# Two-layer relational graph convolution on one core: layer 2's root product made in layer 1, and 21 edge tiles of layer 2 brought by SyncE

## The chip, the cores and the metric

The kernel runs on one core of one Trainium2 chip. The metric is the device time of one execution in microseconds (us). The span of a profile is the time from the first to the last instruction of the profiled execution.

## The reference

The graph has 12,500 nodes with 128 features each and 200,000 edges, sorted by destination; each edge has one of 8 relations. Two layers are computed, and a residual with a layer norm at the end:

```python
def _rgcn_conv(x, src, dst, et, basis, comp, root, bias):
    W = jnp.einsum('rb,bio->rio', comp, basis)
    xw = jnp.einsum('ni,rio->nro', x, W)
    msgs = xw[src, et]
    seg = dst * N_REL + et
    summed = jax.ops.segment_sum(msgs, seg, num_segments=N_NODES * N_REL)
    cnt = jax.ops.segment_sum(jnp.ones((msgs.shape[0],), x.dtype), seg, num_segments=N_NODES * N_REL)
    mean = summed / jnp.maximum(cnt, 1.0)[:, None]
    agg = mean.reshape(N_NODES, N_REL, HIDDEN).sum(axis=1)
    return agg + x @ root + bias
h = x
for l in range(2):
    h_new = jax.nn.relu(_rgcn_conv(h, src, dst, edge_type, basis[l], comp[l], root[l], bias[l]))
    h = h_new + h
out = _layernorm(x + h)
```

The term that the change moves is `x @ root + bias` of the second layer.

## The kernel before

**Tiles, quads and blocks.** The edges are cut into 1,563 tiles of 128. Eight tiles make a quad (`Q = 8`), 196 quads in all (`NQ`). The nodes are cut into 98 blocks of 128 (`NT`). Two quads feed one block.

**Layer 1** runs over the quads `o`. GpSimd (POOL) gathers the source rows of each tile from `x` with one indirect DMA of 128 rows (`gather`, recorded at L806). TensorE multiplies the gathered rows by one-hot matrices that VectorE makes (`means`, L1364), then by the relation weights (`product`, L1396), and puts the result at its place in the block (`place`, L1427 and L1429). `finish` (L1435) adds what was carried over from the block before, makes the next carry with the bias added (L1452), and makes the new block of h with relu and residual (L1472). Each block of h is kept in `hT`, stored to `h_d` by ScalarE's DMA queue, and multiplied by the eight relation weights of layer 2 into rows of `y_d` (`table`, L1495), 51 MB in all.

**Layer 2** runs over the same quads `q`, and reads rows of `y_d`, one per edge. For 130 of the first 192 quads POOL gathers the eight tiles from `y_d`, and TensorE adds them into slots (`slot_sums`, L2026) and puts them in place one quad later (`place_sums`, L2059). The other 62 quads (`ROUTED`: 7, 10, ... 190) are done without a gather of all rows: VectorE compares lists that SyncE loads (`lo_d`, `sc_d`, L1868), TensorE picks rows out of `hT` and sums them (`pick_rows` L1918, `add_up` L1938, `relate` L1958), and POOL brings only one tile of leftovers (`gather_left`, L830). The last four quads go through `add_rows` (L2083). In `place_sums` and `add_rows` the first quad of a block also multiplies the block of h, loaded by SyncE from `h_d` two quads ahead (`open_block`, L1833), by the root weights `w_sb[:, 1, R, :]` (L2063, L2086); this is called `root_in`. The loaded block of h is also the residual in `finish`.

**What sets the order.** `Plan` writes out every engine's instructions by hand, in program order, and adds the semaphore waits that the data needs. Each engine runs its list in order. POOL's gathers are issued `AHEAD = 5` quads before they are used; the rows lie in a ring of 7 quad buffers (`rows_r`). For the last six quads (`LATE = 6`) a gather also waits for the latest sums that TensorE has done (`after`).

**Single rows.** 24 tiles of layer 1 (tile 191 and every 56th after it) aren't gathered by POOL. SyncE (SP) brings their 128 rows with one DMA of 512 bytes each (`single_rows`, L741). The row addresses come from a list in DRAM (`off_d`, made by `single_lists` at two quads, `LISTED = (14, 172)`), 32 of them by one load into SP's registers (L755), each followed by 32 row transfers (L759). A tile is split into eight chunks of 16 rows, put into SP's program at quad `(t - step - 16 + c * step / 8) // 8` for chunk `c` of tile `t`. Its two buffers (`hw_b`) alternate. SP's program also has the loads of layer 2: `fetch` and `fetch_rows` (the lists of the routed quads), `open_block`, the blocks of x, and the stores of the output.

Of the kernel before, what the change touches and what calls it, by code (L numbers as in the profile page):

```python
# [8 lines left out]
F32 = mybir.dt.float32  # L9
# [421 lines left out]
def ordered_path(  # L431
# [78 lines left out]
    NR = len(ROUTED)  # L510
    SORT = 96
    RC, RL = 16, 32
    SINGLES = [("SP", 0, range(191, NQ * Q - 80, 56))]
    SINGLE = {(l, t): (i, k) for i, (_, l, ts) in enumerate(SINGLES) for k, t in enumerate(ts)}
    LISTED = (14, NQ - 24)
    assert all(l == 0 or all(t // Q not in ROUTED and t // Q < NQ - 4 for t in ts) for _, l, ts in SINGLES)
# [13 lines left out]
    y_d = dram.tile([N * R, D], F32, name="y_d")  # L530
    w_d = dram.tile([L, R * D, D], F32, name="w_d")
    h_d = dram.tile([NT, D, P], F32, name="h_d")

    idx = keep([P, B * P], I32, "idx")
    idy = keep([P, B * P], I32, "idy")
# [137 lines left out]
    off = keep([P, B], F32, "off")  # L673
    o2 = keep([P, B], F32, "o2")
    nb_f = keep([1, 1], F32, "nb_f")

    hw_b = {e: [keep([P, D], F32, f"hw_{e}{i}") for i in range(2)] for e in {e: 0 for e, _, _ in SINGLES}}
    offs = [keep([P, len(ts)], I32, f"off{i}") for i, (_, _, ts) in enumerate(SINGLES)]
# [756 lines left out]
    def finish(l, k, apart=False):  # L1435

        n = rows_of(k)

        def first_step():
            a, ac = acc[k] if apart and k + 1 < NT else acc.pop(k)  # L1440
            emits, reads, cells = [], [ac, ("bias_t", l)], []
            if k >= 0:
                vs[k] = a, ac
            if (l, k) == (1, NT - 1):
                return
            if k >= 0:
                t, c = carry.pop(k)
                emits.append(lambda: nc.vector.tensor_add(a[:, :n], a[:, :n], t[:, :n]))  # L1448
                reads.append(c)
            if k + 1 < NT and not apart:  # L1450
                nt, ncell = carry[k + 1] = carry_r.take()
                emits.append(lambda: nc.vector.tensor_scalar(nt, a[:, P:], bias_t[:, l:l + 1], None, op0=ALU.add))  # L1452
                cells.append(ncell)

            vec(in_turn(emits), reads, cells)

        def second_step():
            if k < 0:
                return
            v, vc = vs.pop(k)  # L1460
            h = hT[:, k * P:k * P + n]
            if l == 0:
                res, rc = x_cols(k)
                o, oc = h, h_cells(k)
            else:
                ht, hc = hb.pop(k)
                res, rc = ht[:, :n], [hc]
                g = k * P // GN
                if g not in wide:
                    wide[g] = wide_r.take()  # L1470
                o, oc = wide[g][0][:, k * P % GN:k * P % GN + n], [wide[g][1] + (k,)]
            vec(lambda: nc.vector.scalar_tensor_tensor(o, v[:, :n], 0.0, res, op0=ALU.max, op1=ALU.add),  # L1472
                [vc] + rc, oc)

        def carry_step():
            if k + 1 < NT:
                a, ac = acc[k]
                nt, ncell = carry[k + 1] = carry_r.take()
                vec(lambda: nc.vector.tensor_scalar(nt, a[:, P:], bias_t[:, l:l + 1], None, op0=ALU.add),
                    [ac, ("bias_t", l)], [ncell])  # L1480

        return (first_step, second_step, carry_step)[:3 if apart else 2]


    def table(j):

        n = rows_of(j)
        yr, yrc = yr_r.take()
        split = j >= NT - 2

        def half(k, at_b=None):
            hb, bc = at_b or (s_b[k] if j == NT - 2 else ct_b if split and k == 1 else pt_b)

            def first_step():
                pe(lambda: nc.tensor.matmul(hb[:n].rearrange("p r d -> p (r d)"), hT[:, j * P:j * P + n],  # L1495
                                            w_sb[:, 1, k * H:(k + 1) * H, :].rearrange("p r d -> p (r d)"),
                                            start=True, stop=True),
                   [("h", j)] + [("w", 1, r) for r in range(k * H, (k + 1) * H)], [bc])

            def second_step(copy=copy):  # L1500
                if split and k == 1:
                    vec(lambda: nc.vector.tensor_copy(yr[:n, H:, :], hb[:n]), [bc], [yrc + (k,)])
                else:
                    copy(yr[:n, k * H:(k + 1) * H, :], hb[:n], [bc], [yrc + (k,)])
                if split:
                    load(y_d[j * P * R:(j * P + n) * R, :].rearrange("(p r) d -> p r d", r=R)[:, k * H:(k + 1) * H, :],
                         yr[:n, k * H:(k + 1) * H, :], [yrc + (k,)], [("y_d", j, k)])
                elif k == 1:
                    stores.append(lambda: load(
                        y_d[j * P * R:(j * P + n) * R, :].rearrange("(p r) d -> p (r d)", r=R),  # L1510
                        yr[:n].rearrange("p r d -> p (r d)"), [yrc + (0,), yrc + (1,)], [("y_d", j)], "ACT"))

            return first_step, second_step

        if not split:
            return [lambda at_b, k=k: half(k, at_b) for k in range(2)]
        return [half(0), half(1)]

    todo, turned_to, tables, stores, copies = [], [], [], [], []

# [312 lines left out]
    def open_block(k):  # L1833
        n = rows_of(k)
        t, c = hb_b[k % 3]
        load(t[:, :n], h_d[k][:, :n], [("h_d", k)], new(c))
        hb[k] = t, c

    def spread_of(a):
        return bass.AP(tensor=a.tensor, offset=a.offset, ap=[[0, P], *a.ap])  # L1840
# [197 lines left out]
    def place_sums(q, k, opens, last):  # L2038
        t, c = pl.pop(q)
        o, oc = ys.pop(q)  # L2040
        a, ac = acc[k]
        root_in = opens and k >= 0
        reads = [c, oc]
        m = NW if q in ROUTED else P
        if root_in:
            ht, hc = hb[k]
            reads += [hc, ("w", 1, R)]
        more = []
        if q == SOON // Q:
            reads += fix_rows_c + fix_dm_c  # L2050
            more.append((fix_rows, fix_dm))
        if q in ROUTED:
            i = ROUTED.index(q)
            (lt, lc), (ld, ldc) = left_rows_b[i % len(left_rows_b)], left_dm_b[i % 2]
            reads += [lc, ldc]
            more.append((lt, ld))

        def emit():
            ins = nc.tensor.matmul(a, o[:m], t[:m], start=opens, stop=last and not root_in and not more)  # L2059
            for rows_m, dm_m in more:  # L2060
                ins = nc.tensor.matmul(a, rows_m, dm_m, start=False, stop=last and not root_in)  # L2061
            if root_in:
                ins = nc.tensor.matmul(a[:, :rows_of(k)], w_sb[:, 1, R, :], ht[:, :rows_of(k)], start=False, stop=last)  # L2063
            return ins

        pe(emit, reads, [ac])
        plan.mark("PE")

    def add_rows(q, k, opens, last, between_last=None):
# [1 line left out]
        d, dc = dms.pop((1, q))  # L2071
        a, ac = acc[k]
        n = in_quad(q)
        root_in = opens and k >= 0
        more = []
        if root_in:
            ht, hc = hb[k][0][:, :rows_of(k)], hb[k][1]
            more += [hc, ("w", 1, R)]

        def some(i0, i1):  # L2080
            def emit():
                for i in range(i0, i1):
                    ins = nc.tensor.matmul(a, t[:, i, :], d[:, i, :],  # L2083
                                           start=(opens and i == 0), stop=(last and i == n - 1))
                    if i == 0 and root_in:
                        nc.tensor.matmul(a[:, :rows_of(k)], w_sb[:, 1, R, :], ht, start=False, stop=False)  # L2086
                return ins

            return emit

        if q == NQ - 2:
            for h in range(2):
                pe(some(4 * h, 4 * h + 4), [c + (h,)] + dc + more, [ac, ("done", 1)])
        elif q == NQ - 1:
            m = rows_of(k)
            assert opens and last and k == NT - 1
# [6 lines left out]
                pe(lambda i=i: nc.tensor.matmul(a[:, :m], t[:, i, :], d[:, i, :m], start=False, stop=i == n - 1),  # L2103
                   [c + (i,)] + dc, [ac, ("done", 1)])
        else:
            pe(some(0, n), [c + (0,), c + (1,)] + dc + more, [ac, ("done", 1)])
        plan.mark("PE")

    def first_sums():
# [187 lines left out]
    def end():  # L2297
        for k, step in ending:
            step()
            if k >= 0:  # L2300
                stores.append(lambda k=k: load(h_d[k][:, :rows_of(k)], hT[:, k * P:k * P + rows_of(k)], [("h", k)],
                                               [("h_d", k)], "ACT"))
                tables.extend(table(k))
            if k > 0 and k % TURN == TURN - 1 and k < LATER:
                tables.append(lambda at_b, k=k: turn_rows(k + 1 - TURN, *at_b))
        ending.clear()
# [8 lines left out]
    for o in range(NG - 3):  # L2315
# [37 lines left out]
        for step in behind:  # L2353
            pe(*step)
            plan.mark("PE")
        behind.clear()
        if len(tables) > 4 and (TABLE <= o < SORT - 2 or o >= SORT + NR + 4):
            a, b = tables.pop(0)(pt_b)
            a()
# [50 lines left out]
    opened.clear()  # L2410
    batch(None)
    end()
    placed(g - 4)
    product(g - 3)
    take_product(g - 3)
# [33 lines left out]
        a()  # L2449
    for _, b in halves:  # L2450
        b()

    for q in range(AHEAD):
        gather(1, q)
# [151 lines left out]
```

## Time and profile before

| what | us |
|---|---|
| median of 3 runs | 3384.41 (3383.34 to 3385.06) |
| the profiled execution's own time | 3385.05 |
| its span | 3383.1 |
| time outside the span | 1.95 |
| PE busy | 2766.1 |
| POOL busy | 2547.9 |
| DVE busy | 2270.8 |
| ACT busy | 644.9 |

A row of a group gives line, engine, operation, names of what is written and read, shapes and count, then busy time and the mean of one in ns, then the idle time ahead of it and what ended it. A row of the timeline gives start, duration (both us), engine, line, operation and count; a bracket gives the idle time just before. A row of waits gives the total in us, how often, and the longest. SP's DMA issues stand as SPq. A product of two f32 matrices is recorded as two MATMUL instructions. POOL's time from the start of one gather to the next is its duration plus the 0.30 us in the bracket. Layer 2's first gather starts at 1950.65 us.

### The profile page before, as it was taken

Reading aid. Unit: us, or ns where it says so; the run is one execution under the profiler, and the core shown is the slowest. Engines: PE = TensorE matmul, PEld = TensorE weight load, DVE = VectorE, ACT = ScalarE, POOL = GpSimd, SP = SyncE. Lnnn points to the kernel's source line nnn. Section 1 sums busy time; section 2 is a strip of 40 time slices with the busy share of each in tenths; the row PEclk is TensorE's granted clock in tenths of the full one; section 3 lists DMA queues with packets and bytes.
Section 4 is the critical chain, followed back from the end, with each engine's and each line's share of the span. In section 5 each row is a group of like instructions: output and inputs, shape, how many; then the busy total and the mean of one; then the engine's idle time right before and its main releaser. Section 6 shows DMA issues by size and latency. Waiting matters only on the chain.

```text
span 3383.1 us, 73915 instructions
## 1 busy us (share of the span) xinstructions
PE 2766.1 (82%) x27537; PEld 2228.2 (66%) x27537; DVE 2270.8 (67%) x6302; ACT 644.9 (19%) x1627; POOL 2547.9 (75%) x2677
## 2 busy tenths in 40 slices
PE   6777667877667777777776739999999999999995
PEld 4565565656566666766565627777777777777774
DVE  6665454463367888888333238888888888888884
ACT  1211112222122222222222211111111111111110
POOL 7777777777777777777777777777777777777775
PEclk8999879888888888888988879999999999999997
DMA  4242223443322232222333232233223322333222
GB/s 138 56 59 64 57 77 113 132 130 95 89 82 81 75 89 76 82 77 82 115 105 89 88 101 73 72 84 85 78 78 84 84 78 78 84 85 82 78 78 61
DMA packets 171649, 289.03 MB, mean 85 GB/s; under 512 B 66163, under 2 KB 102813, under 8 KB 171285
## 3 DMA queue, kind: packets, MB, share of 16 engines
q0 software_dynamic: 85408, 175.09, 20.3%
q1 hardware_dynamic: 47146, 50.19, 5.0%
q10 hardware_dynamic: 38731, 58.99, 4.9%
q8 instruction: 218, 3.57, 0.5%
q14 instruction: 146, 1.20, 0.1%
HBM read 218.35 MB, written 65.70 MB: 84 GB/s over the span
## 4 chain that ended last, share of the span: by engine, by line
PE 43%; POOL 40%; issue 13%; DVE 2%; DMA 2%; ACT 1%; POOLq 0%; ACTq 0%; SPq 0%; DVEq 0%
POOL rows L806 40%; PE pt L1918 11%; PE y L1938 9%; PE po L1938 7%; PE po L1958 3%; PE s L2059 3%; PE ct L2026 2%; PE s L1364 2%; PE y L1396 1%; DMA rows<-in_x_dram,idx 1%; PE s L2061 1%; DVE dm L1270 1%; PE s L2063 1%; DVE arena L999 1%; PE pt L1495 0%
## 5 line engine op out<-in xcount | busy, mean ns | idle before, releaser
L806 POOL DMA_INDIRECT rows<-in_x_dram,idx x1539 | 1476.8, 960 | 471.3 <-issue 463.5
L806 POOL DMA_INDIRECT rows<-y_d,idy x1067 | 1010.4, 947 | 325.1 <-issue 316.6
L1364 PE MATMUL s<-dm,rows 128*128 128x128 f32 x3078 | 531.6, 344 | 379.6 <-DMA rows<-in_x_dram,idx 351.8
L1364 PEld LDWEIGHTS s<-dm,rows 128*128 128x128 f32 x3078 | 495.2, 252 | 441.1 <-issue 228.1
L1270 DVE TENSOR_SCALAR dm<-cols,kr,w 128x128 f32<-128x128 f16 x1563 | 525.1, 400 | 194.7 <-PE pt L1495 54.8
L1396 PE MATMUL y<-w_sb,sT 128*128 128x128 f32 x3136 | 438.6, 299 | 46.4 <-ACT sT L704 46.4
L1396 PEld LDWEIGHTS y<-w_sb,sT 128*128 128x128 f32 x3136 | 424.6, 217 | 56.4 <-ACT sT L704 55.2
L1918 PE MATMUL pt<-arena,dm 128*32 128x128 f32 x12152 | 391.3, 275 | 2.8 <-DVE dm L1868 2.1
L704 ACT ACTIVATE sT<-s 128x512 f32<-128x512 f32 x391 | 212.3, 594 | 824.8 <-PE s L1364 824.8
L1918 PEld LDWEIGHTS pt<-arena,dm 128*32 128x32 f32 x12152 | 324.6, 110 | 55.2 <-issue 43.0
L1938 PE MATMUL y<-arena,dm 128*128 128x304 f32 x620 | 229.6, 452 | 35.1 <-DVE arena L1885 35.1
L1229 DVE TENSOR_SCALAR sT<-cols,kr,w 128x32 f32<-128x32 f16 x1040 | 238.1, 300 | 7.4 <-PE s L2063 7.3
L1868 DVE TENSOR_TENSOR dm<-arena,cols 128x768 f32<-128x768 f16 x248 | 231.3, 933 | 4.1 <-DMA dm<-sc_d 3.7
L1448 DVE TENSOR_TENSOR po<-po,carry 128x128 f32<-128x128 f32 x98 | 28.8, 294 | 296.9 <-PE pt L1495 104.2
L1938 PE MATMUL po<-arena,dm 128*128 128x304 f32 x620 | 210.3, 421 | 0.0
L704 ACT ACTIVATE dm<-pt 128x256 f32<-128x256 f32 x248 | 95.4, 385 | 578.2 <-PE pt L1918 533.6
L1495 PE MATMUL pt<-w_sb,arena 128*128 128x512 f32 (+1 forms) x326 | 174.5, 618 | 26.3 <-ACT y_row L704 14.9
L704 ACT ACTIVATE y_row<-pt 128x512 f32<-128x512 f32 x165 | 98.5, 597 | 417.8 <-PE pt L1495 153.3
L1938 PEld LDWEIGHTS y<-arena,dm 128*128 128x128 f32 x620 | 102.9, 189 | 88.4 <-DVE arena L1885 35.3
L1885 DVE TENSOR_SCALAR arena<-cols,comp_sb 128x608 f32<-128x608 f16 x155 | 134.9, 902 | 36.1 <-DMA arena<-y_d,arena 36.0
L1938 PEld LDWEIGHTS po<-arena,dm 128*128 128x128 f32 x620 | 118.4, 191 | 41.3 <-issue 0.7
L1885 DVE TENSOR_SCALAR arena<-cols,sel 128x608 f32<-128x608 f16 x155 | 134.8, 902 | 0.0
(327 smaller groups left out, 3583.5 us busy)
## 6 DMA issues: line engine op xcount, KB each, us to landing
hw_SP<-in_x_dram SPq DMA_DIRECT2D x3072, 0.5 KB
y_d<-y_row ACTq DMA_DIRECT2D x96, 512.0 KB
rows<-in_x_dram,idx POOLq DMA_INDIRECT x1539
rows<-y_d,idy POOLq DMA_INDIRECT x1067
arena<-lo_d SPq DMA_DIRECT2D x62, 256.0 KB
x_g<-in_x_dram SPq DMA_DIRECT2D x24, 512.0 KB
h_d<-arena ACTq DMA_DIRECT2D x96, 64.0 KB
out_dram<-x_g SPq DMA_DIRECT2D x12, 512.0 KB
```

The source lines that it names most:

```text
L704: act(lambda: nc.scalar.activation(out_t, in_t, AF.Copy), reads, writes)
L806: ins.append(nc.gpsimd.indirect_dma_start(out=t[:, i - q * Q, :], out_offset=None, in_=table_t, in_offset=bass.IndirectOffsetOnAxis(ap=ids ...
L1229: vec(in_turn([lambda i=i: nc.vector.tensor_scalar(t[:, i, :], cols[:, :2 * K], kr[:, i0 + i:i0 + i + 1], w[:, i0 + i:i0 + i + 1], op0=ALU ...
L1270: emits.append(lambda i=i: nc.vector.tensor_scalar(t[:, i - q * Q, :wide], cols[:, :wide], ids[:, i:i + 1], w[:, i:i + 1], op0=ALU.is_equa ...
L1364: last = nc.tensor.matmul(s_b[i // 4][0][:, i % 4, :], t[:, i, :] if one is None else one[0], d[:, i, :], start=True, stop=True)
L1396: last = nc.tensor.matmul(y[:m], t[:, r, :nt, :].rearrange("p t k -> p (t k)"), w_sb[:, 0, r, :], start=(r == 0), stop=(r == R - 1))
L1495: pe(lambda: nc.tensor.matmul(hb[:n].rearrange("p r d -> p (r d)"), hT[:, j * P:j * P + n], w_sb[:, 1, k * H:(k + 1) * H, :].rearrange("p ...
L1868: emits = [lambda: nc.vector.tensor_tensor(o[:, :3 * n].rearrange("p (j c) -> p j c", j=3), bits[:, None, u * n:(u + 1) * n].to_broadcast( ...
L1885: vec(lambda v=v, o=o: nc.vector.tensor_scalar(o, segs_p, sg[:, v:v + 1], sg[:, NTL + v:NTL + v + 1], op0=ALU.is_equal, op1=ALU.mult), ["n ...
L1918: last = nc.tensor.matmul(b[k * CAP:(k + 1) * CAP, x, :], o[:n, c:c + CAP], hT[:n, j * P:(j + 1) * P], start=jj == 0, stop=jj == SIZE[g] - 1)
L1938: last = nc.tensor.matmul(b.rearrange("p t d -> p (t d)")[:, :SEG], g[:, x * P:(x + 1) * P], o[:, k * SEG:(k + 1) * SEG], start=v == 0, st ...
L1958: pe(in_turn([lambda r=r: nc.tensor.matmul(b[:NW, 0, :], t_s[:, r * NW:(r + 1) * NW], w_sb[:, 1, r, :], start=r == 0, stop=r == R - 1) for ...
```

## The change

Four things are changed:

- The root product of layer 2 is made in layer 1. For blocks 0 to 96 the new function `rooting` multiplies the block of h by the root weights, ScalarE adds the bias, and its DMA queue stores the result to `hr_d`. At most one such step is done per quad; what is left is done behind the last quad.
- In layer 2 the product is gone from `place_sums` and `add_rows`. `open_block` has SP load the stored product (64 KB, a ring of two buffers) besides the block of h, and `finish` of the block before adds it where it added the bias.
- Block 97 keeps its product (`first_sums`).
- SP's single rows also bring 21 tiles of layer 2 (tile 95 and every 72nd after it, up to 1535), from `y_d`.

```diff
-    SINGLES = [("SP", 0, range(191, NQ * Q - 80, 56))]
+    SINGLES = [("SP", 0, range(191, NQ * Q - 80, 56)), ("SP", 1, range(95, (NQ - 4) * Q, 72))]
...
+    hr_d = dram.tile([NT, D, P], F32, name="hr_d")
...
+    hr_r = Ring(const, 2, [P, P], F32, "hr")
+    hr, rooted = {}, []
...  in finish, first_step
-                emits.append(lambda: nc.vector.tensor_scalar(nt, a[:, P:], bias_t[:, l:l + 1], None, op0=ALU.add))
+                if l == 1 and k + 1 < NT - 1:
+                    rt, rc = hr.pop(k + 1)
+                    emits.append(lambda: nc.vector.tensor_add(nt, a[:, P:], rt))
+                    reads.append(rc)
+                else:
+                    emits.append(lambda: nc.vector.tensor_scalar(nt, a[:, P:], bias_t[:, l:l + 1], None, op0=ALU.add))
...
+    def rooting(k):
+        n = rows_of(k)
+        b, bc = y_full[0][:, 1, :n], y_full[1]
+        t, c = hr_r.take()
+        pe(lambda: nc.tensor.matmul(b, w_sb[:, 1, R, :], hT[:, k * P:k * P + n], start=True, stop=True),
+           [("h", k), ("w", 1, R)], [bc])
+        plan.mark("PE")
+        act(lambda: nc.scalar.activation(t[:, :n], b, AF.Identity, bias=bias_t[:, 1:2]), [bc, ("bias_t", 1)], [c])
+        plan.mark("ACT")
+        stores.append(lambda: load(hr_d[k][:, :n], t[:, :n], [c], [("hr_d", k)], "ACT"))
...  in open_block
+        if k < NT - 1:
+            t, c = hr[k] = hr_r.take()
+            load(t[:, :n], hr_d[k][:, :n], [("hr_d", k)], [c])
...  in place_sums (add_rows alike)
-            if root_in:
-                ins = nc.tensor.matmul(a[:, :rows_of(k)], w_sb[:, 1, R, :], ht[:, :rows_of(k)], start=False, stop=last)
...  in end, then in layer 1's loop
+                if k < NT - 1:
+                    rooted.append(k)
...
+        if rooted:
+            rooting(rooted.pop(0))
...  behind layer 1
+    while rooted:
+        rooting(rooted.pop(0))
+    rooting(NT - 2)
+    for step in stores:
+        step()
+    stores.clear()
```

More of the change, by code (lines that the diff above doesn't have):

```diff
@@ L2041, in place_sums @@
         a, ac = acc[k]
-        root_in = opens and k >= 0
         reads = [c, oc]
         m = NW if q in ROUTED else P
-        if root_in:
-            ht, hc = hb[k]
-            reads += [hc, ("w", 1, R)]
         more = []
@@ L2058, in emit @@
         def emit():
-            ins = nc.tensor.matmul(a, o[:m], t[:m], start=opens, stop=last and not root_in and not more)
+            ins = nc.tensor.matmul(a, o[:m], t[:m], start=opens, stop=last and not more)
             for rows_m, dm_m in more:
-                ins = nc.tensor.matmul(a, rows_m, dm_m, start=False, stop=last and not root_in)
-            if root_in:
-                ins = nc.tensor.matmul(a[:, :rows_of(k)], w_sb[:, 1, R, :], ht[:, :rows_of(k)], start=False, stop=last)
+                ins = nc.tensor.matmul(a, rows_m, dm_m, start=False, stop=last)
             return ins
@@ L2073, in add_rows @@
         n = in_quad(q)
[L2074 to L2078, printed above, removed]
         def some(i0, i1):
@@ L2084, in emit @@
                                            start=(opens and i == 0), stop=(last and i == n - 1))
-                    if i == 0 and root_in:
-                        nc.tensor.matmul(a[:, :rows_of(k)], w_sb[:, 1, R, :], ht, start=False, stop=False)
                 return ins
@@ L2092, in add_rows @@
             for h in range(2):
-                pe(some(4 * h, 4 * h + 4), [c + (h,)] + dc + more, [ac, ("done", 1)])
+                pe(some(4 * h, 4 * h + 4), [c + (h,)] + dc, [ac, ("done", 1)])
         elif q == NQ - 1:
@@ L2105, in add_rows @@
         else:
-            pe(some(0, n), [c + (0,), c + (1,)] + dc + more, [ac, ("done", 1)])
+            pe(some(0, n), [c + (0,), c + (1,)] + dc, [ac, ("done", 1)])
         plan.mark("PE")
@@ L2451, in ordered_path @@
         b()
+    while rooted:
+        rooting(rooted.pop(0))
+    rooting(NT - 2)
+    for step in stores:
+        step()
+    stores.clear()
     for q in range(AHEAD):
```

## Prediction
> **What bounds the kernel now.** I read the page first, then who waited for whom on POOL, then POOL's first and last rows, then stretches of 200 us.
>
> ```profile
> PE 2766.1 (82%) x27537; PEld 2228.2 (66%) x27537; DVE 2270.8 (67%) x6302; ACT 644.9 (19%) x1627; POOL 2547.9 (75%) x2677
> L806 POOL DMA_INDIRECT rows<-in_x_dram,idx x1539 | 1476.8, 960 | 471.3 <-issue 463.5
> L806 POOL DMA_INDIRECT rows<-y_d,idy x1067 | 1010.4, 947 | 325.1 <-issue 316.6
> ```
> ```profile
> POOL rows L806 <- issue: 780.1, 2559, 0.3
> POOL rows L806 <- PE y L1396: 2.1, 7, 0.3
> POOL rows L806 <- PE po L1938: 2.1, 7, 0.3
> ```
> ```profile
> 4.58 1.10 POOL L806 DMA_INDIRECT rows<-in_x_dram,idx  x1 [2.33 <-DMA arena<-in_dst_dram]
> 1950.65 0.94 POOL L806 DMA_INDIRECT rows<-y_d,idy  x1 [0.30 <-issue]
> 3363.68 0.94 POOL L806 DMA_INDIRECT rows<-y_d,idy  x1 [0.31 <-issue]
> ```
> POOL is busy for only 75%, but each gather is followed by 0.3 us of issue, and no wait for another engine is longer than that same 0.3 us. From 4.58 to 3363.68 us POOL issues one indirect DMA after another, through both layers and the seam between them. In layer 2 it issues 1130 of them (1067, 62 leftovers, one fix): 1413.03 us over 1129 intervals, 1.252 us each. A gather taken from POOL is worth 1.25 us, as long as nobody else is late.
>
> ```profile
> 1700.00:1900.00 200.00, 141.26 (x783) 118.86 (x782) 70.11 (x217) 43.99 (x92) 151.23 (x161) 0.85 0.31 94
> 2300.00:2500.00 200.00, 199.22 (x2766) 152.89 (x2766) 171.85 (x439) 29.73 (x87) 151.25 (x161) 1.00 0.30 82
> ```
> ```profile
> 2032.66 1.10 PE L2026 MATMUL ct<-rows,sT 128*32 128x128 f32 x16
> 3333.56 1.10 PE L2026 MATMUL ct<-rows,sT 128*32 128x128 f32 x16 [8.90 <-DMA rows<-y_d,idy]
> ```
> The columns of a stretch are PE, PEld, DVE, ACT and POOL busy, then the clock, the DMA share and GB/s. In layer 1 PE has a quarter of its time to spare; in layer 2 it has none (199.22 of 200). The last two rows are the slot sums of quads 3 and 191: 1300.9 us for 188 quads, 6.92 us each. I count in nine quads, because the new single tiles come every nine: PE needs 62.3 us, POOL 51 issues or 63.8. PE starts five quads behind and catches up only near the end. Both engines must shrink for layer 2 to shrink.
>
> **What leaves PE and POOL.** POOL loses 21 gathers: 21 × 1.252 = 26.3 us, and needs 50 issues or 62.6 us per nine quads.
>
> ```profile
> L2063 PE MATMUL s<-jmp,w_sb 128*128 128x128 f32 x62 | 11.9, 274 | 0.0
> L2063 PE MATMUL s<-id_r,w_sb 128*128 128x128 f32 x62 | 11.9, 274 | 0.0
> L2063 PE MATMUL s<-id_k,w_sb 128*128 128x128 f32 x60 | 11.5, 273 | 0.0
> ```
> Two MATMULs are one root product: 35.3 us for 92, 0.384 us each. The 97 removed ones are 37.2 us, or 4.5 × 0.384 = 1.7 us in nine quads, so PE needs 60.6. VectorE's carry becomes an addition of two tensors instead of a scalar:
>
> ```profile
> L1452 DVE TENSOR_SCALAR carry<-s,bias_t 128x128 f32<-128x128 f32 x93 | 31.7, 341 | 0.0
> L1448 DVE TENSOR_TENSOR s<-s,carry 128x128 f32<-128x128 f32 x93 | 27.2, 292 | 97.0 <-PE s L2059 67.3 <-PE s L2061 29.7
> ```
> By the second row it costs 0.29 instead of 0.34 us; nothing on the path.
>
> **What enters layer 1.** 97 products (37.2 us of PE), 97 ScalarE evictions and 97 issues on ScalarE's queue.
>
> ```profile
> L704 ACT ACTIVATE ys<-ct 128x128 f32<-128x128 f32 x123 | 34.1, 278 | 177.6 <-PE ct L2026 166.6 <-PE po L1938 9.9 <-issue 1.1
> L701 ACTq DMA_DIRECT2D h_d<-arena x96: 325/327/1228, 110.9 to 1946.5; - x96
> PE s L1364 <- DMA rows<-in_x_dram,idx: 340.9, 133, 5.2
> ```
> 97 × 0.28 and 97 × 0.33 are 59 us on ScalarE, busy for 19%. What hides all of it: PE itself waited 340.9 us for gathered rows between 200 and 1900 us, and POOL never waited for PE. I take 0; without that cover it would be 37 us. At the seam `rooting(96)` and the remainders run under a wait that stays:
>
> ```profile
> 2026.40 1.86 DVE L1885 TENSOR_SCALAR arena<-cols,comp_sb 128x608 f32<-128x608 f16 x2 [36.02 <-DMA arena<-y_d,arena]
> ```
> VectorE, and PE behind it, stand for 36 us until POOL has issued quads 0 to 6. The second list (`off_d`, one small DMA at quad 172) falls where SP is idle. I take 0.
>
> **What enters SP in layer 2.** This decides. The price of single rows stands in layer 1, where SP already does them:
>
> ```profile
> L755 SPq TENSOR_LOAD <-off_d x96: 3512/3756/4675, 190.3 to 1758.5; - x96
> 209.49 10.23 SPq L759 DMA_DIRECT2D hw_SP<-in_x_dram  x32
> 223.67 10.71 SPq L759 DMA_DIRECT2D hw_SP<-in_x_dram  x32
> 199.82 100.16 SPq L759 DMA_DIRECT2D hw_SP<-in_x_dram  x220
> 499.88 100.15 SPq L759 DMA_DIRECT2D hw_SP<-in_x_dram  x209
> ```
> 32 addresses take 3.76 us to load, in which SP does nothing else, and their 32 rows 10.2 to 10.7 us; from one batch to the next it is 14.18 us here. Over a stretch without a pause, 220 rows took 100.16 us: 0.455 us a row, 58.3 us a tile. In layer 1 a tile comes due every 56 tiles, at 55 × 1.25 = 69 us: SP has room. In layer 2 it comes due every nine quads, 62.3 us now. The rest of SP's work there:
>
> ```profile
> 1990.40 0.32 SPq L701 DMA_DIRECT2D arena<-lo_d  x1
> 2035.21 0.32 SPq L701 DMA_DIRECT2D jmp<-h_d  x1
> 2035.58 0.42 SPq L701 DMA_DIRECT2D dm<-sc_d  x1
> 2044.72 0.32 SPq L701 DMA_DIRECT2D arena<-lo_d  x1
> 2045.09 0.43 SPq L701 DMA_DIRECT2D id_k<-h_d  x1
> ```
> One issue takes 0.32 us, 0.42 when it follows another, and 0.05 to the next: 0.36 to 0.48. In nine quads there are 3 + 3 lists (0.36), 4.5 blocks of h, 4.5 of the new product, one of x or the output (0.48): 7.0 us. So SP needs 58.3 + 7.0 = 65.3 us, against 62.6 for POOL and 60.6 for PE. **SP becomes the slowest engine**, and it runs in order: behind each chunk stand the lists, the blocks of h and the products that VectorE and PE wait for.
>
> SP can't work ahead: its loads wait for buffers that PE and VectorE release in the same quad (in the rows above it stood from 1990.40 to 2035.21 for a buffer). Before that it does the chunks of quads 0, 2 and 3 unpunished. From 2035.2 us on it is left with five eighths of tile 95 (35 us), 20 tiles (20 × 58.3 = 1166) and the other issues of 185 quads (185/9 × 7.0 = 144): 1345 us. It ends at 3380; the rows land some 2.9 us later, as the last block of h does in the chain of waits:
>
> ```profile
> 3363.24 2.88 DMA id_r<-h_d
> ```
> So quad 191, which needs them, sums at 3383 instead of 3333.56, 49 us late. On the way SP may fall behind: the last chunk of a tile is placed three quads (20.8 us) ahead of its use, less 5.2 us for 16 rows and 2.9 us to land, 13 us. At 5 us lost per nine quads that is used up after some 25 quads.
>
> What is left behind quad 191:
>
> ```profile
> 3342.45 6.72 PE L2083 MATMUL s<-dm,rows 128*128 128x256 f32 x16 [4.50 <-DMA rows<-y_d,idy]
> 3366.68 6.53 PE L2083 MATMUL s<-dm,rows 128*128 128x256 f32 x16
> 3373.04 0.57 PE L2103 MATMUL s<-dm,rows 128*128 128x84 f32 x4
> ```
> Now it is 49.5 us (3333.56 to 3383.1), much of it waiting for POOL. With POOL ahead, PE's own part remains: about 4.4 us to place, 6.7, about 5 and 6.5 for quads 192 to 194, and 9.9 from there to the end: 32.5. Quad 194's gathers still wait for the sums of quad 191, so I take 38, nearer the lower end.
>
> Sum: 3383 + 38 = 3421 us of span, and 1.95 outside: **3423 us**. The profiled execution took 3385.05 and the median is 3384.41, so this is +38 us, 1.1%. Bounds: four batches at 14.18 us are 56.7 us a tile, 20.6 × 1.6 = 33 us less, 3390; at the pace of the other stretch (209 rows in 100.15 us, 61.3 us a tile) 62 us more, 3485. Landing and the rest behind quad 191 are worth −6 to +12 inside that.
>
> The Trainium skill, "Runtime: NRT & Kernel Launch", section "Instruction fetch mechanics", prices a register load at about 200 ns per register. That would be 6.4 us for 32, and 82 batches × 2.6 us would put the sum some 216 us higher, near 3640; the trace has 3.76 us, and the trace decides.
>
> **The rivals.**
>
> *SP is hidden.* If a tile costs SP less than 62.6 − 7.0 = 55.6 us, POOL stays the bound and its 26.3 us are the gain: 3385.05 − 26.3 = 3359. For it: VectorE and PE have lists and blocks loaded two or more quads ahead. Against it: the shortest batch quoted gives 56.7, and slack of 13 us is used once, not per tile. The Trainium skill, "DMA: Bandwidth & Descriptors", section "Issuing engines are not separate DMA queues", speaks for this rival: the sequencer's time to start a DMA "is usually small relative to the DMA itself". Here it is not small: 128 issues and four loads are 58.3 us.
>
> *SP just suffices.* At 56 to 57 us a tile the loss on SP cancels the shorter rest: quad 191 at 3345, the end at 3383, time 3385.
>
> *SP is slower than in the free stretch.* Layer 2 moves 82 GB/s (the stretch at 2300 us above) with broadcast lists on SP's own queue; if rows go at 61.3 us a tile as at 500 us, the time is 3485.
>
> *Nothing moves to SP's account, but layer 1 grows* because `rooting` shares a bank with `product`: up to 37 us. POOL's waits of 0.3 us at most speak against it; I give it no chance of its own.
>
> **How the numbers follow.** SP as bound near the forecast, 3392 to 3455: 0.72. SP still slower, up to 3485: 0.10. Just suffices: 0.06. Hidden, 3355 to 3377: 0.12. A change under 0.2% (7 us) can't be told from none here. So slower 0.82, same 0.06, faster 0.12. The range from 3376 to 3475 leaves out the hidden case and the far end of the slow one; the likeliest case's own range is 3392 to 3455.
>
> **What would show it.** SP's rows from `y_d` without a pause from about 2100 us, its waits for PE and VectorE in layer 2 nearly gone. PE in a stretch of 200 us falls from 199 to about 185 (60.6/65.3), with waits for single rows or for the new product, on PE or on VectorE's carry. POOL gets waits for PE, some 60 us in all, and ends near 3400. Quad 191 sums near 3383. Layer 1 keeps its length: POOL's first gather of layer 2 stays within 5 us of 1950.65. I am wrong if SP's rows have pauses in layer 2, or if a batch of 32 takes under 13.9 us (55.6/4) there.

## Result and profile after

The changed kernel takes 3437.6 us (median of 6, 3431.17 to 3440.53) against 3383.64 us before (3382.11 to 3385.06): ratio 1.0158, interval 1.0144 to 1.0171. The forecast was 3423 (3376 to 3475) with 0.82 for slower. The profiled execution took 3435.26 us, its span is 3433.4. Line numbers have moved: POOL's gathers stand at L810, the register loads of the row addresses at L759, the single rows at L763, SP's other transfers at L705, the slot sums at L2049, the addition of the carry at L1452.

The same groups, waits and stretches as before; columns as there:

```profile
PE 2775.8 (81%) x27537; PEld 2222.2 (65%) x27537; DVE 2266.5 (66%) x6303; ACT 679.5 (20%) x1724; POOL 2522.5 (73%) x2656
L810 POOL DMA_INDIRECT rows<-y_d,idy x1046 | 989.8, 946 | 395.5 <-issue 307.1
```
```profile
DVE s L1452 <- DMA hr<-hr_d: 188.8, 50, 11.2
POOL rows L810 <- PE ct L2049: 80.2, 12, 43.2
PE ct L2049 <- DMA hw_SP<-y_d: 17.2, 2, 16.9
```
```profile
2300.00:2500.00 200.00, 188.71 (x2628) 141.90 (x2621) 160.47 (x411) 28.09 (x82) 151.18 (x161) 0.98 0.32 87
2700.00:2900.00 200.00, 181.89 (x2486) 136.07 (x2475) 155.47 (x402) 27.34 (x80) 142.56 (x152) 0.97 0.31 84
```
POOL has its 21 gathers fewer. Of its idle time in the group 88.4 us is not issue, where it was 8.5 us before; 80.2 us are waits for PE's slot sums, one of them 43.2 us long. In the stretch at 2300 us it still keeps the rhythm of before (151.18 us busy), in the one at 2700 us no longer (142.56). PE is no longer full in these stretches (189 and 182 of 200). VectorE waits 50 times, 188.8 us in all, for the stored product that SP loads; this transfer was not there before. The granted clock is a little lower (0.904 over the span, 0.911 before), but that is not where the time went: it is 0.906 in the experiment step_96 below, which is faster than both kernels.

Then SP's own waits in layer 2, the first three rows of the kernel before (2100 to 3300 us), the others of the changed kernel, same stretch:

```profile
SPq L701 <- DVE dm L1874: 481.9, 54, 11.0
SPq L701 <- PE po L1896: 480.2, 55, 12.3
SPq L701 <- DVE wide L1472: 110.4, 30, 14.4
```
```profile
SPq L705 <- PE pt L1941: 2.6, 7, 0.7
SPq L705 <- DVE dm L1891: 1.0, 3, 0.4
SPq L705 <- DVE iota_f L1236: 0.9, 2, 0.8
```
SP used to wait 1,073 us in its three rows, of 1,200; now nothing holds it up for longer than 0.8 us. Its timeline after, and the last rows that PE needs:

```profile
2345.90 1.19 SPq L763 DMA_DIRECT2D hw_SP<-y_d  x4
2347.14 0.36 SPq L705 DMA_DIRECT2D arena<-lo_d  x1
2347.55 0.42 SPq L705 DMA_DIRECT2D id_k<-h_d  x1
2348.02 0.43 SPq L705 DMA_DIRECT2D hr<-hr_d  x1
2348.49 0.43 SPq L705 DMA_DIRECT2D out_dram<-x_g  x1
2352.95 10.30 SPq L763 DMA_DIRECT2D hw_SP<-y_d  x32
2363.35 0.32 SPq L705 DMA_DIRECT2D dm<-sc_d  x1
...
3387.55 5.12 SPq L763 DMA_DIRECT2D hw_SP<-y_d  x16
```
```profile
3393.76 0.88 PE L2049 MATMUL ct<-rows,sT 128*32 128x128 f32 x11 [16.92 <-DMA hw_SP<-y_d]
```
Issue follows issue; the only gap (2348.9 to 2352.9) is the register load of 32 addresses. The last 16 rows start at 3387.55, and quad 191, which summed at 3333.56 before, sums at 3393.76, 60 us later, after waiting 16.92 us for a single tile's rows (`hw_SP`). From the start of the third register load of layer 2 (2037.0 us) to that of the 84th (3377.5) are 81 batches: 16.55 us each, with all other issues of SP between. In nine quads, which is four batches, that is 66.2 us, against POOL's 62.6. Added up from SP's records between these two loads, each counted to the start of the next: the 81 register loads 317 us, their 2,592 rows 866 us, all other issues 158 us. So a tile costs SP 58.4 us, and the other issues 7.8 us in nine quads.

### The profile page after: what moved, and what is told of

Same layout as the page of the kernel before. It is cut to its first block, busy times and chain, and to the rows that moved or that the text cites. A ratio compares the mean times of both kernels' runs of the same rounds, so it can differ in the third digit from the quotient of the medians.

```text
span 3433.4 us, 79877 instructions
## 1 busy us (share of the span) xinstructions
PE 2775.8 (81%) x27537; PEld 2222.2 (65%) x27537; DVE 2266.5 (66%) x6303; ACT 679.5 (20%) x1724; POOL 2522.5 (73%) x2656
## 4 chain that ended last, share of the span: by engine, by line
POOL 37%; PE 26%; issue 14%; SPq 12%; DVE 7%; DMA 3%; ACT 1%; POOLq 0%; ACTq 0%; DVEq 0%
POOL rows L810 37%; SPq L763 7%; PE pt L1941 6%; PE y L1961 5%; PE po L1961 4%; SPq L759 4%; PE po L1981 2%; PE s L2078 2%; PE s L1368 2%; SPq L705 2%; DMA hr<-hr_d 1%; PE y L1400 1%; PE ct L2049 1%; DVE dm L1274 1%; DMA rows<-in_x_dram,idx 1%
## 5 line engine op out<-in xcount | busy, mean ns | idle before, releaser
L810 POOL DMA_INDIRECT rows<-in_x_dram,idx x1539 | 1472.1, 957 | 471.8 <-issue 464.8
L810 POOL DMA_INDIRECT rows<-y_d,idy x1046 | 989.8, 946 | 395.5 <-issue 307.1
L1368 PE MATMUL s<-dm,rows 128*128 128x128 f32 x3078 | 519.1, 338 | 373.8 <-DMA rows<-in_x_dram,idx 354.2
L1368 PEld LDWEIGHTS s<-dm,rows 128*128 128x128 f32 x3078 | 483.5, 246 | 432.8 <-issue 235.5
L1400 PE MATMUL y<-w_sb,sT 128*128 128x128 f32 x3136 | 446.9, 304 | 28.1 <-ACT sT L708 28.0
L1400 PEld LDWEIGHTS y<-w_sb,sT 128*128 128x128 f32 x3136 | 433.1, 221 | 34.7 <-ACT sT L708 33.8
L1941 PE MATMUL pt<-arena,dm 128*32 128x128 f32 x12152 | 401.8, 280 | 62.3 <-DVE dm L1891 42.1
L1941 PEld LDWEIGHTS pt<-arena,dm 128*32 128x32 f32 x12152 | 334.3, 112 | 128.7 <-issue 122.6
L1452 DVE TENSOR_TENSOR po<-po,carry 128x128 f32<-128x128 f32 x98 | 28.9, 295 | 317.9 <-PE po L1431 114.8
L1452 DVE TENSOR_TENSOR s<-s,carry 128x128 f32<-128x128 f32 x97 | 28.8, 297 | 234.2 <-DMA hr<-hr_d 188.8
```

What stands on the lines that cost most here:

```text
L810: ins.append(nc.gpsimd.indirect_dma_start(out=t[:, i - q * Q, :], out_offset=None, in_=table_t, in_offset=bass.IndirectOffsetOnAxis(ap=ids ...
L1368: last = nc.tensor.matmul(s_b[i // 4][0][:, i % 4, :], t[:, i, :] if one is None else one[0], d[:, i, :], start=True, stop=True)
L1400: last = nc.tensor.matmul(y[:m], t[:, r, :nt, :].rearrange("p t k -> p (t k)"), w_sb[:, 0, r, :], start=(r == 0), stop=(r == R - 1))
L1941: last = nc.tensor.matmul(b[k * CAP:(k + 1) * CAP, x, :], o[:n, c:c + CAP], hT[:n, j * P:(j + 1) * P], start=jj == 0, stop=jj == SIZE[g] - 1)
```

## Experiments

Theory A is the prediction's: SP's issue time bounds layer 2. Theory B: the added load of the product comes too late by itself. Theory C: the single rows' traffic slows the other transfers, whoever issues them. Ratios are against the kernel before on the same chip (3382.34 us for the first four, 3380.53 for the last four); the 3437.6 us of the changed kernel are those above.

**One half of the change each: root_only**

```diff
-    SINGLES = [("SP", 0, range(191, NQ * Q - 80, 56)), ("SP", 1, range(95, (NQ - 4) * Q, 72))]
+    SINGLES = [("SP", 0, range(191, NQ * Q - 80, 56))]
```


> The changed kernel without its 21 single tiles in layer 2; the root products stay in layer 1, and SyncE loads the stored product besides h. Theory A (SyncE's issue time is the bound of layer 2 in the changed kernel, because of the 2,688 single rows): POOL is the bound again with 51 issues in nine quads, so the time is that of the kernel before, 3384 +-4 us, and the wait of VectorE's carry for the stored product (188.8 us after) is gone. Theory B (the added load of the product comes too late by itself, two quads ahead of its use): the wait stays and the time stays above 3420 us. Theory C (the single rows' traffic slows the other transfers): as A, 3384 us.

3380.7 us, ratio 0.9996 (0.9986 to 1.0005). No wait for the stored product is left. The root product's move costs nothing that these runs can tell, layer 1's 97 products included, and by itself brings nothing: POOL has as many gathers as before. B falls: the same load, at the same place, is in time when SP is free.

**singles_only**: the kernel before with the new `SINGLES` line.

> The kernel before with the 21 single tiles of layer 2, and nothing else changed: the root product stays in layer 2, no stored product is loaded. Theory A: SyncE saves 94 loads of 0.48 us, 45 us, of the changed kernel's work, so its last rows come near 3347 us and the end near 3389: time 3391 (3380 to 3405), SyncE still without pauses over most of layer 2. Theory B: without the stored product there is no late load, POOL gains 26 us and PE's 62.3 us in nine quads decide: about 3362 us. Theory C: the traffic of the single rows is the same, so the time stays near 3435 us.

3380.35 us, ratio 0.9992 (0.9982 to 1.0001), at the lower end of A's range and far from B and C. SP is still without pauses (from 2100 to 3300 us it waits 0.6 us at the longest): its batch takes 15.86 us (81 batches from 2040.1 to 3324.7 us), the last rows come at 3339.5. That is 63.4 us in nine quads, near the 63.8 of POOL before, so the gain of 26 us in POOL is eaten up. Waits of this kernel in layer 2:

```profile
POOL rows L806 <- PE ct L2026: 26.4, 6, 24.9
PE s L2059 <- DMA id_r<-h_d: 16.7, 4, 10.7
PE ct L2026 <- DMA hw_SP<-y_d: 3.1, 1, 3.1
```
The difference from the changed kernel is larger than expected, and gives the product's price: 81 × (16.55 − 15.86) = 56 us for the 91 loads that lie in these batches of the changed kernel, 0.61 us each on average and not 0.48. The row of these loads there (minimum, median and maximum in ns):

```profile
L705 SPq DMA_DIRECT2D hr<-hr_d x97: 417/425/1510, 1981.1 to 3395.9; - x97
```
By the median, with 0.05 us to the next, the price is the expected 0.48. But ten of the 91 took 0.88 to 1.51 us, so that the 91 come to 52 us; what held these ten up is not shown. SP's semaphore instructions, 100 in the changed kernel's batches and 19 here, make the other 4 us.

**Fewer single tiles: step_96**

```diff
-    SINGLES = [("SP", 0, range(191, NQ * Q - 80, 56)), ("SP", 1, range(95, (NQ - 4) * Q, 72))]
+    SINGLES = [("SP", 0, range(191, NQ * Q - 80, 56)), ("SP", 1, range(95, (NQ - 4) * Q, 96))]
```


> The changed kernel with every 96th tile of layer 2 instead of every 72nd: 16 single tiles instead of 21, one in twelve quads. Theory A: SyncE needs 58 + 9.5 us in twelve quads, POOL 67 issues or 83.9 us; SyncE has room, POOL is the bound again and has 16 x 1.25 = 20 us less than before: 3364 us (3358 to 3370), the wait for the stored product gone. Theory B: the load of the product is as late as before: above 3420 us. Theory C: 16/21 of the traffic, so about 16/21 of the loss: 3425 us.

3360.75 us, ratio 0.9936 (0.9920 to 0.9953): faster than both kernels, as A has it. POOL's row in the groups names issue and a few us of PE; among the waits, PE has none for single rows, and SP has long ones again:

```profile
L810 POOL DMA_INDIRECT rows<-y_d,idy x1051 | 994.9, 947 | 320.4 <-issue 311.2 <-PE po L1961 3.0 <-PE pt L1941 2.1
```
```profile
SPq L705 <- DVE dm L1897: 148.0, 50, 5.7
```

**The same traffic with half the issues: pairs.** One transfer writes two partitions from one row; the kernel leaves out the rows of the odd edges of these tiles, and puts the even edge's row in their place.

```diff
-    return [by[e].dma_start(b[c * RC + j:c * RC + j + 1, :], bass.AP(
-        tensor=t8.tensor, offset=offsets[e][a + j], ap=[[4 * D, 1], [1, 4 * D]]))
-        for j in range(RC)]
+    m = 1 + l
+    return [by[e].dma_start(b[c * RC + j:c * RC + j + m, :], bass.AP(
+        tensor=t8.tensor, offset=offsets[e][a + j], ap=[[0 if l else 4 * D, m], [1, 4 * D]]))
+        for j in range(0, RC, m)]
...
-    lane="sr" if e == "SP" else "ar", n=RC)
+    lane="sr" if e == "SP" else "ar", n=RC // (1 + l))
```


> The changed kernel with half as many SyncE issues for the same traffic in layer 2: one transfer writes two partitions with 512 bytes each, both from the row of the even edge (the odd edges of these tiles get the wrong row). Addresses, register loads, bytes and row reads are as many as after. Theory A: a tile costs SyncE 4 x (3.8 + 16 x 0.35 + 0.4) = 39 us instead of 58, with the rest 46 of POOL's 62.6 us in nine quads: POOL is the bound, 3385 - 26 = 3359 us (3352 to 3366). Theory B: nothing changes for the product's load: 3437 us. Theory C: the same traffic, so 3430 us or more.

3356.02 us, ratio 0.9917 (0.9901 to 0.9934). The bytes and the row reads are those of the changed kernel, only the issues are halved, and the whole gain of 26 us appears. SP waits for buffers again, 222 us between 2100 and 3300 us for VectorE to free the buffer `dm` alone. C falls. The issue rows of this kernel:

```profile
L764 SPq DMA_DIRECT2D hw_SP<-in_x_dram x3072: 227/228/949, 190.3 to 1817.3; - x192
L764 SPq DMA_DIRECT2D hw_SP<-y_d x1344: 236/237/693, 1990.3 to 3285.4; - x192
```
Minimum, median and maximum in ns: a transfer of two rows costs SP 237 where one of a single row costs 228. For these rows SP pays per transfer, not per byte.

**More lead for the product: hr_early**

```diff
-    hr_r = Ring(const, 2, [P, P], F32, "hr")
+    hr_r = Ring(const, 3, [P, P], F32, "hr")
...  in open_block
-        if k < NT - 1:
-            t, c = hr[k] = hr_r.take()
-            load(t[:, :n], hr_d[k][:, :n], [("hr_d", k)], [c])
+        for j in ((k, k + 1) if k == 0 else (k + 1,)):
+            if j < NT - 1:
+                t, c = hr[j] = hr_r.take()
+                load(t, hr_d[j], [("hr_d", j)], [c])
```


> The changed kernel with the stored product loaded one block (two quads, 14 us) earlier, in a ring of three buffers; nothing else. Theory A (SyncE's throughput is the bound): SyncE has the same work, its last rows come at about 3392 us again, the wait only moves from VectorE's carry to the single rows: 3437 us (3428 to 3441). Theory B (the added load is issued too late): 14 us more lead take the 11.2 us of the longest wait away, and POOL is the bound: about 3360 us.

3436.59 us, ratio 1.0164 (1.0147 to 1.0181): nothing gained, and SP's last rows start at 3394.0 us, 3392.4 in the changed kernel. The wait named loudest in the changed kernel is gone, and others took its place:

```profile
PE ct L2050 <- DMA hw_SP<-y_d: 78.4, 17, 24.7
DVE dm L1892 <- DMA arena<-lo_d: 64.8, 22, 6.4
DVE s L1452 <- DMA hr<-hr_d: 5.1, 1, 5.1
```
Whatever comes from SP is late; in these two kernels, which consumer notices first is a matter of lead.

**Fewer other issues on SP: one_load, then lists_act.** In the first, `h_d` and `hr_d` are halves of one tensor `hh_d`, and one transfer loads both, into a ring of three new buffers. The second also moves the 62 small lists:

```diff
...  in open_block
-        load(t[:, :n], h_d[k][:, :n], [("h_d", k)], new(c))
...
-            t, c = hr[k] = hr_r.take()
-            load(t[:, :n], hr_d[k][:, :n], [("hr_d", k)], [c])
+            load(t, hh_d[k], [("h_d", k), ("hr_d", k)], new(c))
...  lists_act, in fetch_rows
-    load(t[:2 * NTL], sc_d[i]..., [("sc_d", i)], new(c))
+    load(t[:2 * NTL], sc_d[i]..., [("sc_d", i)], new(c), "ACT")
```


> The changed kernel with h and the stored product of a block side by side in one DRAM tensor, so that one SyncE transfer of 128 KB brings both: 94 issues fewer, the same bytes. Theory A: a batch of 32 rows with all that stands between takes 15.86 us as in the run without the product's loads, instead of 16.55, so the last rows come near 3340 us and the end near 3380: 3381 us (3374 to 3388), SyncE still without pauses. Theory B: the product comes no earlier in SyncE's program than before, 3420 us or more. Theory C (traffic): unchanged, 3437 us.

> As the kernel with one load of h and product, and the 62 small lists (sc_d) go through ScalarE's queue instead of SyncE's. Theory A: 62 x 0.4 = 25 us less for SyncE, its last rows near 3315 us; then POOL's 50 issues decide again, 26 us less than before: 3360 us (3354 to 3368). Theories B and C: no change against the kernel with one load.

3382.24 us, ratio 1.0006 (0.9996 to 1.0016), then 3357.58 us, ratio 0.9932 (0.9915 to 0.9948). Both as A has it: 94 issues fewer bring the loss back to nothing, 62 more away bring the gain, 24.7 us or 0.40 us an issue. In the first the waits for SP's transfers are still there; in the second POOL hardly waits any more (the first two rows are one_load's, the others lists_act's):

```profile
DVE s L1452 <- DMA hh<-hh_d: 120.0, 39, 10.9
POOL rows L810 <- PE ct L2050: 27.7, 2, 27.4
```
```profile
DVE s L1452 <- DMA hh<-hh_d: 56.6, 22, 8.8
POOL rows L810 <- PE ct L2050: 3.0, 2, 2.7
```
SP still has no pause in lists_act: between 2100 and 3300 us it waits 0.5 us at the longest, and its batch takes 15.61 us (80 batches from 2050.2 to 3299.3 us). That is 62.5 us in nine quads, level with POOL's 62.6. Its last rows start 25.8 us earlier than in one_load (3313.6 against 3339.4), about the gain.

The transfers are the same in number and bytes in these two kernels; only the queue that issues 62 of them differs. The Trainium skill ("DMA: Bandwidth & Descriptors", section "Issuing engines are not separate DMA queues") says that spreading transfers over engines only saves the sequencer's time to start them. The runs agree, by the 24.7 us above, and here that time was the bound.

**Twice as many register loads: rl_16**

```diff
-    RC, RL = 16, 32
+    RC, RL = 16, 16
```


> The changed kernel with 16 addresses per register load instead of 32, in both layers: twice as many loads, the same rows. The load of one register took 0.476 us before and one of 32 takes 3.79, so one of 16 should take 2.1 us and two of them 4.2, with 0.1 us more to start: 0.5 us more for 32 rows. Theory A: 84 x 0.5 = 42 us later, 3479 us (3465 to 3490). If a load's price were fixed, near 3.8 us whatever it brings, 84 x 3.9 = 330 us later. Theories B and C: no change, 3437 us.

3468.15 us, ratio 1.0261 (1.0244 to 1.0278): 30.6 us more than the changed kernel, where 42 were expected and a fixed price would have meant 330. SP's last rows come 30.5 us later. The loads of the changed kernel, then of this one:

```profile
L759 SPq TENSOR_LOAD <-off_d x180: 3543/3787/13059, 190.1 to 3377.5; - x180
```
```profile
L759 SPq TENSOR_LOAD <-off_d x360: 1869/2024/7974, 188.7 to 3415.6; - x180
```
Two loads of 16 take 4.05 us by the medians, 0.26 more than one of 32; 84 batches make 22 of the 30.6 us. The rest is in the means, which lie 0.1 us above the medians for both kinds of load, and there are twice as many loads of 16: over 81 batches of layer 2 the loads last 345.3 us instead of 314.8, 30.5 more, and with the gaps behind them 33.0 more. The expectation had taken the slope from a single load of one register.

## Why the prediction was right

- **POOL as the bound before, 1.25 us a gather:** right. When SP has room, 16 tiles bring 21.6 us (step_96) and 21 bring 26.3 (pairs).
- **Nothing in layer 1:** right. POOL's first gather of layer 2 started at 1946.44 us (1950.65 before), and root_only is level with the kernel before.
- **SP becomes the slowest engine:** right, shown from five sides: fewer tiles, fewer issues for the same bytes, fewer loads, lists on another queue, and dearer loads all moved the time the way SP's work moved, and more lead did not.
- **SP's total:** forecast 65.3 us in nine quads, measured 66.2. A tile with its register loads was right (58.4 us against 58.3); a batch of 32 alone is 14.6 us of it, above the 13.9 that would have refuted the forecast. The term that was too small is the other issues, 7.8 us instead of 7.0, most of it the product's load with its 0.61 us instead of 0.48. Over 82 batches the total makes 19 us. About 4 us of it came back because SP had done one chunk more at the start, and over 1 because nothing stands behind the last batch: SP's rows ended at 3392.7 instead of 3380. A slip of 1 us in the sum is beside the point: five eighths of tile 95 are 36 us at 58.3 a tile, not 35.
- **Landing:** quad 191 summed 1.1 us after SP's last issue, where 3 were allowed, so it came 10.8 us late (3393.76 for 3383).
- **Behind quad 191:** forecast 38 us, measured 39.6 (3393.76 to 3433.4). The number is right, partly by luck: quads 192 to 194 take PE 3.7, 5.9 and 3.7 us instead of 6.7, about 5 and 6.5, and waits for VectorE and for the last block of h, which were not in the sum, fill the rest.
- **Sum:** 10.8 us at quad 191 and 1.6 behind it are the 12.4 between the forecast span of 3421 and the measured 3433.4. The median of the six runs lies 2.3 us above the profiled one. That the total came within 15 us is in part that misses of both signs were added.
- **Who waits:** the lead of 13 us was worked out for the single rows only. The product of the next block ran out of lead first (188.8 us on VectorE's carry against 17.2 for the rows). It made no difference to the time, as hr_early shows. POOL's waits for PE came to 80 us where some 60 were expected, and its last gather started at 3409 us instead of near 3400.
- **The rivals:** SP as hidden (3359) is what the kernel does once SP has fewer transfers to issue (pairs 3356.02, step_96 with its fewer tiles 3360.75); lists_act (3357.58) has the same time with SP just level with POOL. SP just sufficing (3385) is what singles_only and one_load do, at 63.4 and 63.8 us in nine quads. SP slower than in the free stretch (3485) rested in part on a misreading: the pace at 500 us is partly a wait. SP stood there once, for 3.6 us, until PE's products of `means` (L1364) had freed a buffer; between 200 and 300 us it had no wait. Layer 2's rows, at 58.4 us a tile, show no slower pace.

## What to carry to other kernels

When work is moved to an idle queue, add up that queue's issue time over the stretch in which it will run, its other transfers and register loads included, and compare it with the pace of the engine that is relieved; here SP waited 1,073 of 1,200 us before, and what was added still made it slower than POOL (66.2 us against 62.6 in nine quads). A named wait on a transfer may only be the first to notice an engine that is late with everything: give it more lead and see whether the time moves. Here, merging 94 pairs of transfers gave back the whole loss, and moving 62 more to another queue brought 24.7 us.

## Hardware behaviour that was not expected

- A register load on SP took 3.787 us for 32 registers and 2.024 for 16, by the medians of 180 and 360 loads: 0.110 us for each register between the two. Drawn on to one register that line gives 0.37 us, and the one such load of SP in the kernel before took 0.476.
- SP's time to issue a transfer depended on what stood ahead of it, and hardly on its size. A row took 228 ns with 512 bytes, and 237 with twice that. A load of 64 KB of h (singles_only) took 355 ns straight behind a row and 425 behind a list `lo_d`; a load of 128 KB (one_load) took the same 355 and 425 in these two places (medians of 26 to 30).
